# Graph convolution stage of a four-layer graph network: the product of gathered rows moved to the head of the iteration, the steps behind it one block later, reciprocal roots taken for two blocks at once

## The chip, the cores and the metric

The kernel runs on one core of one Trainium2 chip. The metric is the device time of one execution in microseconds (us), lower is better; the time before is the median of three runs.

## The reference, cut to what matters

A residual stream `x` of 4096 nodes by 256 features passes through four graph layers over one sparse 4096 x 4096 adjacency. The stage of this case computes layer 1 and prepares layer 2:

```python
h = jnp.maximum(_layernorm(x, axis=-1), 0.0)
# layer 1: graph convolution
adj_hat = adj + jnp.eye(N)
adj_norm = adj_hat / jnp.sum(adj_hat, axis=1, keepdims=True)
x = x + jnp.tanh(adj_norm @ (h @ W) + b)
# layer 2: attention over the neighbours, four heads
h = jnp.maximum(_layernorm(x, axis=-1), 0.0)
Wh = (h @ W2.T).reshape(n, HEADS, D_K)          # and the scores Wh . a_l, Wh . a_r
```

## The kernel before, in words

The nodes are cut into 32 blocks of 128 rows (`NB = 32`, `P = 128`, `D = 256`). A block's row of the adjacency has few nonzero columns, so for each block it is packed into five chunks of 128 columns (`CHUNKS + 1`): four chunks of neighbours anywhere in the graph and the block's own diagonal chunk. Two neighbouring blocks share one spare chunk (`acx`, 64 rows for each). The matching rows of `h @ W` lie in DRAM (`v_d`), and four indirect DMAs a block, one a chunk, fetch them, plus one for the spare of two blocks (`vgx`). So the 32 blocks need 144 indirect DMAs. They are issued by GpSimd (POOL), all on line 889.

The kernel runs stage by stage: attention (layer 0) up to 2180 us, the graph convolution from about 2195 to 2445 us, the second attention layer up to about 2720 us, and a last sparse product up to the end. The diff touches the graph convolution. Its loop runs over `b`, with one block entering each turn. A turn of before does this, with `o = b - LAG` and `LAG = 2`:

- loads of `xr` (the stream), `ac`, `acx` and the block's own rows of `v_d` from SyncE's queue (SP), and the gathers `vg`, `vgx` from POOL. The pool `gcnadj` holds six buffers of each.
- `second.normalise(o)` (L2238, L2243): ScalarE (ACT) makes `h` of block `o`, TensorE (PE) transposes it into `pt`.
- `second.product(o - 1)` (L2254): PE multiplies the transposed `ht` by `w_gat` into `pv`.
- `across_targets(o - 3)` (L2297 to L2300): PE transposes 4 columns of `steep`, ACT copies them to `steep_t`, SP stores them.
- `second.turned(o)` (L2248): VectorE (DVE) copies `pt` to `ht`.
- `sparse_product` (L920, L921): PE multiplies the packed adjacency of block `b` by the gathered rows into `acc`.
- `second.store(o - 1)` (L2282 to L2292): three exponentials on ACT, two instructions on DVE, the store to `table_d`.
- `y` (L2334 on DVE, tanh L2337 on ACT), `masks` (L2338, L2340), the sum into `xr` (L2342) and `second.stats(b)` (L2209 to L2232) with the reciprocal root of the variance by Newton steps: 13 small DVE instructions with the shift.

The order of DVE, ACT and PE is the program's own (`manual_schedule` over those three). A scheduler places SP's and POOL's instructions. Each engine works its list in order. The second attention layer gathers from `table_d`, so its first gather waits for the last stores of this stage.

Of the kernel before, what the change touches and what calls it, by code (L numbers as in the profile page):

```python
# [63 lines left out]
F32 = mybir.dt.float32  # L64
BF16 = mybir.dt.bfloat16
I32 = mybir.dt.int32
U32 = mybir.dt.uint32
# [9 lines left out]
P = 128  # L77
N = 4096
D = 256
NB = N // P  # L80
DC = D // P
DA = 64
HEADS = 4
# [582 lines left out]
def fast_layers(  # L666
# [80 lines left out]
    v_d = [dram.tile([N + 1, D], F32, name=f"v{k}_d") for k in range(2)]  # L747
# [152 lines left out]
    def gathered(pool, v_d, b, width=0):  # L900

        v = pool.tile([P, CHUNKS + 1, max(width, v_d.shape[1])], F32, name="vg")[:, :, : v_d.shape[1]]
        nc.sync.dma_start(v[:, CHUNKS, :], v_d[b * P : (b + 1) * P, :])
        for k in range(CHUNKS):
            gather(v[:, k, :], v_d, main_index(column, k, b))
        return v
# [10 lines left out]
    def sparse_product(acc, b, ac, v, acx, vx):  # L917

        for k in range(CHUNKS + 1):
            nc.tensor.matmul(acc, ac[:, k, :], v[:, k, :], start=(k == 0), stop=False)  # L920
        nc.tensor.matmul(acc, acx[side(b)], vx[side(b)], start=False, stop=True)  # L921
# [6 lines left out]
    sm = layer0.enter_context(tc.tile_pool(name="sm", bufs=4))  # L928
    wk = layer0.enter_context(tc.tile_pool(name="wk", bufs=2))
    ps = layer0.enter_context(tc.tile_pool(name="ps", bufs=2, space=PSUM))  # L930
# [1214 lines left out]
    with ExitStack() as st:  # L2145
# [3 lines left out]
        with tc.manual_schedule(engines=MANUAL):  # L2149
            enter1(va1, s1, vg_pool)  # L2150
            for b in range(-1, NB + 4):
                period1(b)
                if b == -1:
                    for q in range(8):
                        bs = slice(q * NB // 8, (q + 1) * NB // 8)
# [18 lines left out]
    w_last = weights(res, last_w, "w_last")  # L2174

    w_gat = res.tile([P, DC, D + 2 * HEADS], F32, name="w_gat")
# [15 lines left out]
    scale = res.tile([P, NB], F32, name="scale")  # L2192
# [4 lines left out]
    class Projection:  # L2197


        def __init__(self, sm, wk, ps, w, put, group, width=D):  # L2200
            self.group = group
            self.sm, self.wk, self.ps, self.w, self.put, self.width = sm, wk, ps, w, put, width
            self.tiles = {}

        def stats(self, b):


            six = self.sm.tile([P, 6], F32, name="six")
            nc.vector.bn_stats(six, xr[:, b, :])  # L2209
            nc.vector.bn_aggr(spread_[:, b, :], six)  # L2210
            if b % self.group < self.group - 1:
                return
            bs = slice(b + 1 - self.group, b + 1)
            var = self.sm.tile([P, self.group], F32, name="var")
            nc.vector.tensor_scalar_add(var, spread_[:, bs, 1], LN_EPS)
            if self.group > 1:
                nc.gpsimd.tensor_tensor(scale[:, bs], var, minus_half[:, : self.group], op=ALU.pow)
                return
            y, t = scale[:, bs], self.sm.tile([P, 1], F32, name="t")
            bits = self.sm.tile([P, 1], U32, name="bits")  # L2220
            nc.vector.tensor_scalar(bits, var.bitcast(U32), 1, None, op0=ALU.logical_shift_right)
            nc.vector.tensor_scalar(y.bitcast(U32), bits, -1.0, 1597463007.0, op0=ALU.mult, op1=ALU.add)
            for _ in range(3):
                nc.vector.tensor_mul(t, y, y)
                nc.vector.scalar_tensor_tensor(t, t, -0.5, var, op0=ALU.mult, op1=ALU.mult)
                nc.vector.scalar_tensor_tensor(y, t, 1.5, y, op0=ALU.add, op1=ALU.mult)
            self.shifts(b)

        def shifts(self, b):
            if b % self.group == 0:  # L2230
# [31 lines left out]
    def to_table(wk, v_d):  # L2262
        def put(b, pv):
            v = wk.tile([P, D], F32, name="v")
            nc.scalar.copy(v, pv)
            nc.sync.dma_start(v_d[b * P : (b + 1) * P, :], v)

        return put
# [3 lines left out]
    with ExitStack() as st:  # L2272
        adj_pool = st.enter_context(tc.tile_pool(name="gcnadj", bufs=6))
        sm = st.enter_context(tc.tile_pool(name="gcnsm", bufs=4))
        wk = st.enter_context(tc.tile_pool(name="gcnwk", bufs=3))
        ps = st.enter_context(tc.tile_pool(name="gcnps", bufs=2, space=PSUM))

        def put(b, pv):
            tab = wk.tile([P, TW], F32, name="tab")
            heads = tab[:, :HW].rearrange("p (h d) -> p h d", h=HEADS)  # L2280
            sr = pv[:, D + HEADS :]
            nc.scalar.activation(heads[:, :, DK], sr, AF.Exp, scale=SLOPE)  # L2282
            nc.scalar.activation(tab[:, HW:], sr, AF.Exp, scale=1.0 - SLOPE)
            nc.scalar.activation(steep[:, b, :], pv[:, D : D + HEADS], AF.Exp, scale=1.0 - SLOPE)
            nc.vector.tensor_copy(scores[:, b, :], pv[:, D:])
            nc.vector.tensor_tensor(
                heads[:, :, :DK],
                pv[:, :D].rearrange("p (h d) -> p h d", h=HEADS),
                heads[:, :, DK:].to_broadcast([P, HEADS, DK]),
                op=ALU.mult,  # L2290
            )
            nc.sync.dma_start(table_d[b * P : (b + 1) * P, :], tab)  # L2292

        def across_targets(b):

            pt = ps.tile([HEADS, P], F32, name="pst", tag="pv")
            nc.tensor.transpose(pt, steep[:, b, :], ident)  # L2297
            t = wk.tile([HEADS, P], F32, name="steep_t")
            nc.scalar.copy(t, pt)
            nc.sync.dma_start(steep_d[b], t)  # L2300

        second = Projection(sm, wk, ps, w_gat, put, 1, D + 2 * HEADS)
        LAG = 2
        with tc.manual_schedule(engines=MANUAL):
            for b in range(NB + LAG + 3):
                o = b - LAG
                if b % 4 == 0 and b < NB:
                    for c in (0, 4) if b == 0 else (b + 4,):
                        if c < NB:
                            nc.sync.dma_start(xr[:, c : c + 4, :], blocks(x1_d)[:, c : c + 4, :])  # L2310
                if b < NB:
                    ac = adj_pool.tile([P, CHUNKS + 1, P], F32, name="ac")
                    nc.sync.dma_start(ac, adjc_d[b])
                    if b % 2 == 0:
                        acx = adj_pool.tile([P, P], F32, name="acx")
                        nc.sync.dma_start(acx, adjx_d[b // 2])
                        vx = gathered_spare(adj_pool, v_d[0], b)
                    vg = gathered(adj_pool, v_d[0], b)
                if 0 <= o < NB:
                    second.normalise(o)  # L2320
                if 0 <= o - 1 < NB:
                    second.product(o - 1)
                if 0 <= o - 3:
                    across_targets(o - 3)
                if 0 <= o < NB:
                    second.turned(o)
                if b < NB:
                    acc = ps.tile([P, D], F32, name="acc")
                    sparse_product(acc, b, ac, vg, acx, vx)
                if 0 <= o - 1 < NB:  # L2330
                    second.store(o - 1)
                if b < NB:
                    y = wk.tile([P, D], F32, name="y")
                    nc.vector.scalar_tensor_tensor(  # L2334
                        y, acc, rdeg[:, b : b + 1], bias, op0=ALU.mult, op1=ALU.add
                    )
                    nc.scalar.activation(y, y, AF.Tanh)  # L2337
                    nc.vector.tensor_scalar(masks[:, b], ac, 0.0, None, op0=ALU.is_gt)  # L2338
                    if b % 2:
                        nc.vector.tensor_scalar(masks_x[:, b // 2], acx, 0.0, None, op0=ALU.is_gt)  # L2340

                    nc.vector.scalar_tensor_tensor(  # L2342
                        xr[:, b, :], y, -1.0, xr[:, b, :], op0=ALU.add, op1=ALU.add
                    )
                    second.stats(b)
        nc.vector.tensor_reduce(
            mild, scores.rearrange("p b k -> p (b k)"), AX.X, ALU.max, apply_absolute_value=True
        )
        nc.vector.tensor_scalar(mild, mild, SCORE_MAX, None, op0=ALU.is_le)
# [3 lines left out]
    with ExitStack() as st:  # L2353
        tab_pool = st.enter_context(tc.tile_pool(name="gattab", bufs=5))
        u_pool = st.enter_context(tc.tile_pool(name="gatu", bufs=2))
        sm = st.enter_context(tc.tile_pool(name="gatsm", bufs=4))
        wk = st.enter_context(tc.tile_pool(name="gatwk", bufs=3))
        ps = st.enter_context(tc.tile_pool(name="gatps", bufs=2, space=PSUM))
        third = Projection(sm, wk, ps, w_last, to_table(wk, v_d[1]), 2)
        state = [{} for _ in range(NB)]  # L2360
        LAG = 6

# [92 lines left out]
        with tc.manual_schedule(engines=MANUAL):  # L2455
            for b in range(NB + LAG + 2):
                o = b - LAG
# [54 lines left out]
    with ExitStack() as st:  # L2512
        adj_pool = st.enter_context(tc.tile_pool(name="lastadj", bufs=6))
        wk = st.enter_context(tc.tile_pool(name="lastwk", bufs=3))
# [79 lines left out]
```

## Time and profile before

| what | before |
|---|---|
| median of three runs | 2910.83 us (2905.03 to 2912.14) |
| profiled execution, its own time | 2910.45 us |
| its span in the profile | 2908.7 us |
| busy in the span | PE 87%, DVE 80%, ACT 68%, POOL 38% |
| first gather of the stage starts | 2198.52 us |
| `y` of the first, second, last block starts | 2218.50, 2225.90, 2430.02 us |
| last gather of the stage starts | 2391.86 us |
| first gather of the next stage starts | 2444.68 us |

The busy shares are those of the whole span; they say little of this stage, which takes a twelfth of it. The stage is read from its own window: the waits in it, the order of time of one turn, and the pace of the gathers. PE's clock is granted in stretches at full or half speed; "PEclk" is the mean granted share.

### The profile page before, as it was taken

The numbers are of one execution on the slowest core, as the hardware profiler recorded it, in microseconds if no ns is written. First come the engines' busy times: TensorE is split into PE (matmuls) and PEld (weight loads), VectorE is DVE, ScalarE is ACT, GpSimd is POOL, SyncE is SP. The second block draws the span as 40 slices with busy tenths as digits, with TensorE's granted clock in tenths as the row PEclk, the third lists the DMA queues.
The fourth block names the chain that finished last, engine by engine and source line by source line (L and its number), as shares of the span: only waits on it lengthen the run. The fifth ranks groups of instructions, "written<-read, shape, count | busy, mean of one in ns | idle before, by whom it ended". The sixth has DMA issues, their size and how long they took to land. (4 is left out here: it accounts for less than half of the span.)

```text
span 2908.7 us, 43850 instructions
## 1 busy us (share of the span) xinstructions
PE 2523.0 (87%) x12359; PEld 1850.5 (64%) x12359; DVE 2312.7 (80%) x9516; ACT 1976.6 (68%) x3289; POOL 1098.0 (38%) x1152
## 2 busy tenths in 40 slices
PE   5769999999999884699999999999895776999777
PEld 4537777777777762467676766677773554788444
DVE  4799999999999866898989879999964765888200
ACT  2689999999999634887888878788520123999100
POOL 3200000000000001488888554344425752764476
PEclk7779999999999996899999999999996887999887
DMA  7611222222222113244444433334337653654576
GB/s 254 222 55 59 92 69 87 89 69 91 80 75 89 40 40 103 64 126 126 122 136 118 134 111 102 99 117 123 101 98 227 209 165 104 173 164 121 160 210 183
DMA packets 227371, 349.57 MB, mean 120 GB/s; under 512 B 34727, under 2 KB 160172, under 8 KB 227116
## 3 DMA queue, kind: packets, MB, share of 16 engines
q1 hardware_dynamic: 185820, 237.70, 25.7%
q0 software_dynamic: 40320, 108.72, 13.6%
q8 instruction: 101, 1.65, 0.2%
q14 instruction: 154, 1.26, 0.1%
q10 hardware_dynamic: 976, 0.23, 0.0%
HBM read 280.22 MB, written 66.28 MB: 119 GB/s over the span
## 5 line engine op out<-in xcount | busy, mean ns | idle before, releaser
L1269 ACT ACTIVATE unread<-e,next_pair 128x4096 uint8<-128x4096 f32 (+1 forms) x320 | 859.5, 2686 | 160.9 <-DVE next_pair L1365 109.0
L1619 PE MATMUL pa<-va,at 128*128 128x256 f32 x2048 | 495.2, 387 | 0.0
L1619 PE MATMUL pa<-h,at 128*128 128x256 f32 x2048 | 469.0, 379 | 0.1
L1619 PEld LDWEIGHTS pa<-va,at 128*128 128x128 f32 x2048 | 376.4, 193 | 65.4 <-issue 21.6
L1619 PEld LDWEIGHTS pa<-h,at 128*128 128x128 f32 x2048 | 376.6, 190 | 45.3 <-issue 0.5
L1483 DVE MAX8 best<-near 128x8 f32<-128x256 f32 x1024 | 394.6, 415 | 0.1
L1610 ACT COPY at<-pat 128x512 f32<-128x512 f32 x512 | 284.0, 577 | 135.3 <-PE pat L1604 135.1
L1236 PE MATMUL pl<-kt,qb 64*128 64x512 f32 x1024 | 280.4, 657 | 91.3 <-ACT e L1250 88.4
L1604 PE MATMUL pat<-ident,e 128*128 128x128 f32 x2048 | 305.0, 279 | 51.2 <-DVEq L1543 25.1
L1604 PEld LDWEIGHTS pat<-ident,e 128*128 128x128 f32 x2048 | 240.0, 142 | 139.1 <-DVEq L1543 47.8
L1485 POOL COPY eighth<-best 128x16 f32<-128x16 f32 x64 | 47.1, 736 | 722.7 <-DVE best L1483 711.7
L1250 ACT ACTIVATE e<-pl,minus_guess 128x1024 f32<-128x1024 f32 x256 | 284.3, 1125 | 26.8 <-PE pl L1236 26.7
L1475 DVE SCALAR_TENSOR_TENSOR near<-e,end_hi 128x4096 f32<-128x4096 f32 x64 | 286.6, 4477 | 0.1
L1535 DVE SCALAR_TENSOR_TENSOR e<-e,end_t 128x4096 f32<-128x4096 f32 x64 | 286.2, 4472 | 0.2 <-issue 0.2
L889 POOL DMA_INDIRECT vg<-v_d,column x256 | 243.4, 951 | 91.0 <-issue 67.7
L920 PE MATMUL acc<-vg,ac 128*128 128x256 f32 x640 | 215.9, 489 | 66.3 <-DMA vg<-v_d,column 29.6
L920 PEld LDWEIGHTS acc<-vg,ac 128*128 128x128 f32 x640 | 146.9, 247 | 132.1 <-issue 59.8
L1236 PEld LDWEIGHTS pl<-kt,qb 64*128 64x128 f32 x1024 | 89.8, 194 | 195.7 <-ACT e L1250 156.4
L889 POOL DMA_INDIRECT vg<-mixed_d,column x128 | 180.5, 1410 | 57.6 <-issue 32.4
L2407 PE MATMUL acc<-u,tabg 128*65 128x128 f32 x1280 | 170.2, 280 | 13.5 <-DVE u L2397 13.5
L889 POOL DMA_INDIRECT vg<-far_d,column x128 | 166.6, 1301 | 39.0 <-issue 38.1
L2394 ACT ACTIVATE u<-targets,tabg 128x128 f32<-128x128 f32 x544 | 162.1, 389 | 10.0 <-DMA targets_x<-steep_d 10.0
(608 smaller groups left out, 4427.7 us busy)
## 6 DMA issues: line engine op xcount, KB each, us to landing
adj<-in_adjt SPq DMA_DIRECT2D x128, 512.0 KB
ac<-adjc_d SPq DMA_DIRECT2D x64, 320.0 KB
adjc_d<-ac SPq DMA_DIRECT2D x32, 320.0 KB
vg<-v_d SPq DMA_DIRECT2D x64, 128.0 KB
targets<-steep_d SPq DMA_DIRECT2D x32, 256.0 KB
ac<-adjc_d SPq DMA_DIRECT2D x32, 256.0 KB
table_d<-tab SPq DMA_DIRECT2D x32, 132.0 KB
tabg<-table_d SPq DMA_DIRECT2D x32, 132.0 KB
```

The source lines that it names most:

```text
L889: nc.gpsimd.indirect_dma_start(out, None, rows, bass.IndirectOffsetOnAxis(ap=index, axis=0))
L920: nc.tensor.matmul(acc, ac[:, k, :], v[:, k, :], start=(k == 0), stop=False)
L1236: nc.tensor.matmul(pl[:, r, :], s["qb"][rows], kt[rows, j * 512 : (j + 1) * 512], start=True, stop=True,)
L1250: nc.scalar.activation(s["e"][:, j * 1024 : (j + 1) * 1024], pl.rearrange("p r c -> p (r c)"), AF.Exp, bias=minus_guess[:, b : b + 1], acc ...
L1269: nc.scalar.activation(unread[:, :width], s["e"][:, :width], func, bias=s["at"], scale=-1.0, accum_out=s["signs"] if func == AF.Sign else ...
L1475: nc.vector.scalar_tensor_tensor(near, s["e"], end["hi"][:, b : b + 1], s["e"], op0=ALU.is_lt, op1=ALU.mult, accum_out=s["low"])
L1483: nc.vector.max(best[:, k, :], near[:, k * (N // SEG) : (k + 1) * (N // SEG)])
L1535: nc.vector.scalar_tensor_tensor(s["e"], s["e"], last, s["e"], op0=ALU.is_ge, op1=ALU.mult, accum_out=s["held"])
L1604: nc.tensor.transpose(pt[:, k, :], s["e"][:, c * P : (c + 1) * P], ident)
L1610: nc.scalar.copy(at, s["pt", g])
L1619: nc.tensor.matmul(s["pa"], s["at", g][:, k, :], va[:, c, :D], start=(c == 0), stop=(c == NB - 1))
L2407: nc.tensor.matmul(s["acc"][:, h, :], s["tab"][:, k, h * (DK + 1) : (h + 1) * (DK + 1)], s["u"][:, k, h, :], start=(k == 0), stop=False,)
```

## The change

In a turn, the sparse product of block `b` comes first on PE, ahead of the transposition, the product and the small transposition of earlier blocks. Those now lag three blocks behind instead of two. `y` and the masks come ahead of `turned` and `store` on DVE, and `tanh` ahead of the three exponentials on ACT. The Newton steps work on two columns, once every two blocks.

```diff
-        def __init__(self, sm, wk, ps, w, put, group, width=D):
-            self.group = group
+        def __init__(self, sm, wk, ps, w, put, newton, width=D):
+            self.group, self.newton = 2, newton
...
-            if self.group > 1:
+            if not self.newton:
                 nc.gpsimd.tensor_tensor(scale[:, bs], var, minus_half[:, : self.group], op=ALU.pow)
                 return
-            y, t = scale[:, bs], self.sm.tile([P, 1], F32, name="t")
-            bits = self.sm.tile([P, 1], U32, name="bits")
+            y, t = scale[:, bs], self.sm.tile([P, self.group], F32, name="t")
+            bits = self.sm.tile([P, self.group], U32, name="bits")
...
-            self.shifts(b)
+            self.shifts(bs.start)
...
-        second = Projection(sm, wk, ps, w_gat, put, 1, D + 2 * HEADS)
-        LAG = 2
+        second = Projection(sm, wk, ps, w_gat, put, True, D + 2 * HEADS)
+        LAG = 3
...
+                if b < NB:
+                    acc = ps.tile([P, D], F32, name="acc")
+                    sparse_product(acc, b, ac, vg, acx, vx)
                 if 0 <= o < NB:
                     second.normalise(o)
                 if 0 <= o - 1 < NB:
                     second.product(o - 1)
                 if 0 <= o - 3:
                     across_targets(o - 3)
-                if 0 <= o < NB:
-                    second.turned(o)
-                if b < NB:
-                    acc = ps.tile([P, D], F32, name="acc")
-                    sparse_product(acc, b, ac, vg, acx, vx)
-                if 0 <= o - 1 < NB:
-                    second.store(o - 1)
                 if b < NB:
                     y = wk.tile([P, D], F32, name="y")
...
                     if b % 2:
                         nc.vector.tensor_scalar(masks_x[:, b // 2], acx, 0.0, None, op0=ALU.is_gt)
+                if 0 <= o < NB:
+                    second.turned(o)
+                if 0 <= o - 1 < NB:
+                    second.store(o - 1)
+                if b < NB:
                     nc.vector.scalar_tensor_tensor(
                         xr[:, b, :], y, -1.0, xr[:, b, :], op0=ALU.add, op1=ALU.add
                     )
                     second.stats(b)
...
-        third = Projection(sm, wk, ps, w_last, to_table(wk, v_d[1]), 2)
+        third = Projection(sm, wk, ps, w_last, to_table(wk, v_d[1]), False)
```

The instance `third` of the next stage keeps its two-block groups and its power on POOL; only the way it is asked for differs.

## The prediction, made before the changed kernel ran

> **What bounds the stage now.** I read the page for the share of the stage, then the waits inside it, then one turn in order of time, then the gathers, and last the same gathers in the kernel's final stage. The waits from 2210 to 2440 us (engine and line, what it waited for, us in total, times, longest):
>
> ```profile
> ACT y L2337 <- DVE y L2334: 148.1, 32, 35.4
> PEld pt L2243 <- ACT h L2238: 64.5, 32, 2.8
> DVE y L2334 <- PE acc L921: 54.4, 32, 8.6
> PE pt L2243 <- ACT h L2238: 51.2, 32, 2.4
> POOL vg L889 <- PE acc L920: 16.3, 11, 2.8
> PEld acc L920 <- DMA vg<-v_d,column: 4.1, 4, 2.4
> ```
>
> PE stands 51.2 us for `h`, 1.6 us in each turn, and almost never for a gather (4.1 us). POOL stands 16.3 us for PE to free a buffer. So PE's own chain sets the pace and the gathers run ahead of it. One turn shows the chain: PE first, then ACT over the same time.
>
> ```profile
> 2397.49 0.44 PE L2243 MATMUL pt<-ident,h 128*128 128x128 f32 x2 [1.58 <-ACT h L2238]
> 2397.77 1.06 PE L2254 MATMUL pv<-w_gat,ht 128*128 128x264 f32 x4
> 2398.66 0.27 PE L2297 MATMUL pst<-ident,steep 128*4 128x128 f32 x1
> 2398.77 2.32 PE L920 MATMUL acc<-vg,ac 128*128 128x256 f32 x10
> 2401.03 0.70 PE L921 MATMUL acc<-vgx,acx 64*128 64x256 f32 x2
> 2403.30 0.44 PE L2243 MATMUL pt<-ident,h 128*128 128x128 f32 x2 [1.58 <-ACT h L2238]
> ...
> 2402.34 0.42 ACT L2337 ACTIVATE y<-y 128x256 f32<-128x256 f32 x1 [2.89 <-DVE y L2334]
> 2402.66 0.59 ACT L2238 ACTIVATE h<-xr,shift,scale 128x256 f32<-128x256 f32 x1
> ```
>
> `acc` ends at 2401.73, DVE makes `y`, ACT its tanh, and only then `h`: `h` is behind tanh in ACT's list, although its data was ready long before. Then PE goes on at 2403.30. PE's work in a full-clock turn is 2397.49 to 2401.73 = 4.24 us; the turn takes 5.81. With the half-clock stretches the mean turn is (2430.02 - 2225.90) / 30 = 6.80 us over blocks 1 to 31.
>
> What comes next is the gathers. The windows of the stage, its end, and the final stage (PE, PEld, DVE, ACT, POOL busy, then PEclk, DMA share, GB/s):
>
> ```profile
> 2210.00:2392.00 182.00, 137.53 (x477) 95.88 (x476) 121.86 (x546) 33.00 (x141) 128.13 (x135) 0.82 0.71 218
> 2392.00:2430.00 38.00, 30.09 (x109) 21.10 (x107) 25.48 (x116) 7.12 (x34) 0.81 (x1) 0.85 0.09 31
> 2740.00:2880.00 140.00, 107.94 (x293) 62.85 (x292) 10.62 (x25) 0.00 (x0) 105.85 (x113) 0.78 0.73 217
> ```
>
> POOL's last gather starts at 2391.86; for 38 us more PE works off blocks that have landed. In the final stage, with the same 144 gathers and little PE work, the start of the first is 2719.15 and of the last:
>
> ```profile
> 2898.26 0.95 POOL L889 DMA_INDIRECT vg<-v_d,column  x1 [0.30 <-issue]
> 2902.99 0.42 DVE L2527 SCALAR_TENSOR_TENSOR y<-acc,xr 128x256 f32<-128x256 f32 x1 [4.62 <-PE acc L921]
> ```
>
> That is (2898.26 - 2719.15) / 143 = 1.2525 us a gather (0.95 busy, 0.30 between), 5.64 us a block of 4.5 gathers, and 4.7 us from the start of the last gather to the use of its block. This is the floor under the changed stage.
>
> **The change, part by part.** *The product first.* After the change PE has, in the 1.6 us in which it waited for `h`, the next block's product, which needs only gathered rows and a PSUM buffer that `y` of two blocks ago has freed. `h` comes at the head of ACT's turn, behind the exponentials of the turn before; its shift was finished a whole turn earlier. After PE's last step of a turn (`pst`), ACT has steep_t 0.26, tanh 0.42, three exponentials of about 0.15 and `h` 0.59, about 1.7 us, while PE has 2.9 us (full clock) of sparse product ahead of the next `pt`. So no wait on `h` is left. The whole wait would be worth up to 51 us, but the gathers allow less. Without any wait for PE, the last of the 144 starts at 2198.52 + 143 x 1.2525 = 2377.6, and the last `y` at 2382.3 by the final stage's 4.7 us. PE must also do pt, pv and pst between blocks; I add 1.7 us and take 2384. It was 2430.0: 46 us earlier.
>
> Does PE keep that pace? 4.24 us at full clock; at half clock about 8.2 (the product 2227.86 to 2233.36 = 5.5, pt to pst 2435.41 to 2438.07 = 2.7). At half clock for every second stretch the mean is 2 / (1/4.24 + 1/8.2) = 5.6 us, just the gathers' pace; at the stage's own 0.82 it is about 5.2. Here a rule speaks against the change. The trace shows the clock at 0.82 although PE's longest steady wait is 2 us. The Trainium skill, TensorE: Matmul & The Clock Gate, "HAM oscillation", asks only that no idle gap exceed some 3.4 us, by which the clock would be 1.0 and a turn 4.24; its section "A second HAM failure mode" says that frequent short idling makes the clock swing, and the change turns one gap a turn into several short waits for gathers. The trace sides with the second: the final stage, with such waits, has 0.78. By either rule PE needs 4.2 to 5.6 us and the sum stays; only a clock that stays half breaks it.
>
> *DVE.* 13 small instructions at about 0.19 us from start to start now run 16 times, not 32: 208 fewer, 40 us of DVE time. That is off the path: DVE waits 54.4 us for `acc` already. What it does on the path: in an odd turn DVE has y 0.48, masks 0.70, ht 0.42, then stands for the exponentials (behind pst, steep_t and tanh, 2.5 to 3.8 us after `acc` ends), then 0.15 + 0.41 + 0.43 + 0.61 and 2.5 of Newton: 6.5 to 7.8 us. The even turn has no Newton: 4 to 5.3. The pair, 10.5 to 13.1, stands against 11.3 of gathers; the upper end is for half clock throughout. `y` of the even block comes a little late, but PE needs its buffer only two products later. I cost this at nothing, and 13.1 / 2 = 6.55 if the cover fails.
>
> *SP and POOL.* The stores of block j move from turn j+3 to j+4 in SP's list (`steep` from j+5 to j+6). Loads behind them are 6 blocks ahead of use, so a turn's delay leaves over 4 turns; landing takes about 3.7 us for a gather. Cost nothing; POOL's list is unchanged but for a few spare gathers that stand a place or two earlier, behind a product that is six blocks old by then. The Trainium skill, GPSIMD Engine Reference, "Key points", warns that DVE instructions with two SBUF inputs (the sum into `xr` is one) contend with GpSimd: the gather mean is 0.954 us here and 0.947 the median of the final stage without DVE work, so 1 us in 144; I use the measured one.
>
> *The end.* The stage before needs 14.66 us from the last `y` (2430.02) to the next stage's first gather (2444.68). Now `y` to shift takes 6.7 instead of 4.64 (ht, scores and tab come ahead of the sum into `xr`, and wait for the exponentials), and two blocks, not one, have `h` behind that shift: one more pass of pt, pv, pst, 1.5 to 2.7 us, I take 2.1. So 14.66 + 2.1 + 2.1 = 18.9.
>
> *Sum.* 2384 + 18.9 = 2402.9 for the next stage's first gather instead of 2444.68: 41.8 us less. Nothing behind it is changed, and it starts with that gather, so the rest shifts whole. Against the profiled execution's 2910.45: 2868.7. That execution is 0.4 us from the median, so the figure stands for the median too.
>
> **The rivals.** *PE or the landings at 6.2 us a block* instead of 5.64: for it, the clock's swings and the nearness of 5.6 to 5.64; against it, a PE that is behind is never idle and so regains its clock. From block 5 (about 2240) 26 blocks at 6.2 give 2402, the next gather at 2421, 24 us less: 2887. Chance 0.10.
>
> *The wait is hidden anyway*: DVE's odd and even turns bind at 6.55 us, 8 us less over 31 turns, and the longer end returns 4: 2907, no change to be seen (0.3% is 8.7 us, about what a measurement of this kernel can tell). Against it: 13.1 holds only at half clock. Chance 0.04.
>
> *Half clock throughout, slower*: place, PE's short waits for single gathers; price, 8.2 us a block from block 2 (2231) gives 2469 for the last `y`, 2488 for the next gather, +43: 2954. It decides once over 78% of the time is at half clock (mean above 6.8, clock under 0.61). For it: 2196 to 2231 ran mostly at half clock with such waits. Against it: the final stage's 0.78. Chance 0.06.
>
> **How the numbers follow.** The forecast (0.80) is 2869, its own range 2862 (last gather used at once, end as before: -48) to 2878. Faster: 0.80 + 0.10; same 0.04; slower 0.06. The range 2860 to 2886 takes in the forecast and most of the first rival.
>
> **What would show it.** Right: PE no longer waits for `h`, but for gathers of `v_d`; gathers at 1.25 us without a wait for PE to the last, near 2378; last `y` near 2384; next stage's first gather near 2403; clock 0.75 to 0.9. Wrong: POOL still waiting for `acc` (PE is the bound), `y` spaced by 6.5 in pairs of unequal turns (DVE), a clock near 0.5, or a gather gap above 1.25.

## The result, and the profile after

The changed kernel takes 2869.89 us (median of four runs, 2865.41 to 2874.15) against 2911.05 us of the kernel before (four runs, 2905.03 to 2912.14): a ratio of 0.9863, with a 95% interval of 0.9842 to 0.9883, or 41.2 us less. The forecast was 2869.

The profiled execution of the changed kernel took 2874.15 us, its span is 2872.4. It is the longest of the four, 4 us over their median, so it shows 36 us less than the profile of before. Read by stages, the change of this stage is 40.0 us:

| start, us | before | after | predicted |
|---|---|---|---|
| first gather of the stage | 2198.52 | 2199.75 | |
| last gather of the stage | 2391.86 | 2381.03 | 2377.6 |
| last `y` | 2430.02 | 2386.68 | 2384 |
| first gather of the next stage | 2444.68 | 2405.96 | 2402.9 |
| first to last gather | 193.3 | 181.3 | 179.1 |
| last `y` to the next stage's first gather | 14.66 | 19.3 | 18.9 |
| first gather of the stage to first of the next | 246.2 | 206.2 | 204.4 |

The first gather comes 1.2 us later than before, and what lies behind the stage takes 466.4 us instead of 464.0. The change touches neither; these 3.7 us are less than the 8.7 us by which the four runs of the changed kernel differ.

The waits of the stage come first, as they did for before (engine and line, what it waited for, us in total, times, longest; 2200 to 2400 us). Only the waits that bear on the chain are shown:

```profile
PEld acc L920 <- DMA vg<-v_d,column: 33.8, 40, 2.0
POOL vg L889 <- issue: 31.4, 103, 0.3
DVE y L2330 <- PE acc L921: 22.6, 16, 2.9
PE acc L920 <- DMA vg<-v_d,column: 17.7, 27, 1.6
PEld pt L2243 <- ACT h L2238: 7.5, 5, 3.3
PE pt L2243 <- ACT h L2238: 5.3, 3, 2.9
POOL vg L889 <- PE acc L920: 1.5, 5, 0.3
```

PE's wait for `h` has fallen from 51.2 us in 32 turns to 5.3 us in three. In its place PE now waits for gathers, 17.7 us, and its weight load 33.8. (PE's multiplications and its weight loads, PEld, wait at the same time; the two sums overlap.) POOL has no stall: each of its entries is 0.3 us, the plain gap between two gathers, and the 16.3 us for which it waited for `acc` are down to five such gaps. So PE now follows the gathers, and they run to the end without waiting for PE:

```profile
2199.75 1.02 POOL L889 DMA_INDIRECT vgx<-v_d,column  x1 [16.25 <-DVE found L1594]
...
2381.03 0.95 POOL L889 DMA_INDIRECT vg<-v_d,column  x1 [0.30 <-issue]
...
2386.68 0.45 DVE L2330 SCALAR_TENSOR_TENSOR y<-acc,rdeg,bias 128x256 f32<-128x256 f32 x1
...
2405.96 0.94 POOL L889 DMA_INDIRECT tabg_x<-table_d,column  x1 [23.98 <-DMA steep_d<-steep_t]
```

One turn in order of time shows the new chain. It begins at the end of a block's product:

```profile
2329.81 0.61 ACT L2238 ACTIVATE h<-xr,shift,scale 128x256 f32<-128x256 f32 x1
2331.03 0.70 PE L921 MATMUL acc<-vgx,acx 64*128 64x256 f32 x2
2331.65 0.44 PE L2243 MATMUL pt<-ident,h 128*128 128x128 f32 x2
2331.93 1.06 PE L2254 MATMUL pv<-w_gat,ht 128*128 128x264 f32 x4
2332.82 0.27 PE L2297 MATMUL pst<-ident,steep 128*4 128x128 f32 x1
2332.93 0.61 PE L920 MATMUL acc<-vg,ac 128*128 128x256 f32 x2
2333.34 0.41 ACT L2333 ACTIVATE y<-y 128x256 f32<-128x256 f32 x1
...
2334.37 1.39 PE L920 MATMUL acc<-vg,ac 128*128 128x256 f32 x4 [0.83 <-DMA vg<-v_d,column]
...
2336.57 1.64 PE L920 MATMUL acc<-vg,ac 128*128 128x256 f32 x4 [0.81 <-DMA vg<-v_d,column]
```

`h` ends at 2330.42, before the product of this turn does. `pt` follows the product at once, without a bracket of idle time; before, it stood there for 1.58 us. The stop is now inside the next product, twice 0.8 us, each for a chunk of gathered rows. The window of the stage, with PE, PEld, DVE, ACT, POOL busy, PEclk, DMA share and GB/s, shows 548 matmuls in 170 us, where before had 477 in 182, and a higher clock (0.88, not 0.82):

```profile
2210.00:2380.00 170.00, 147.96 (x548) 95.80 (x549) 109.19 (x426) 34.80 (x160) 129.16 (x135) 0.88 0.78 237
```

### The profile page after: what moved, and what is told of

It reads as the page before. It is cut to its first block, busy times and chain, and to the rows that moved or that the text cites. A ratio compares the mean times of both kernels' runs of the same rounds, so it can differ in the third digit from the quotient of the medians.

```text
span 2872.4 us, 43628 instructions
## 1 busy us (share of the span) xinstructions
PE 2512.8 (87%) x12359; PEld 1838.6 (64%) x12359; DVE 2281.8 (79%) x9308; ACT 1973.6 (69%) x3289; POOL 1099.9 (38%) x1152
## 3 DMA queue, kind: packets, MB, share of 16 engines
q14 instruction: 153, 1.25, 0.1%
## 5 line engine op out<-in xcount | busy, mean ns | idle before, releaser
L1604 PE MATMUL pat<-ident,e 128*128 128x128 f32 x2048 | 306.2, 280 | 51.2 <-DVEq L1543 25.4
L920 PEld LDWEIGHTS acc<-vg,ac 128*128 128x128 f32 x640 | 133.0, 228 | 156.3 <-DMA vg<-v_d,column 72.8
L2408 PE MATMUL acc<-u,tabg 128*65 128x128 f32 x1280 | 170.5, 280 | 13.8 <-DVE u L2398 13.8
```

The lines of the kernel that those rows point to most:

```text
L1604: nc.tensor.transpose(pt[:, k, :], s["e"][:, c * P : (c + 1) * P], ident)
L2408: nc.tensor.matmul(s["acc"][:, h, :], s["tab"][:, k, h * (DK + 1) : (h + 1) * (DK + 1)], s["u"][:, k, h, :], start=(k == 0), stop=False,)
```

## The experiments

The change has three parts: the order of the turn, the lag with it, and the reciprocal roots of two blocks at once. The first set of four runs asks which of them carries the 41 us, and whether the order is needed as a whole. A second and a third set test the new bound. The medians of the first set are of four runs (`e2`: 20), in ratio to 23 runs of before (2909.60 us, 2900.81 to 2917.14).

**The order alone.** The changed kernel with a lag of two blocks and one root a turn, as before:

```diff
-            self.group, self.newton = 2, newton
+            self.group, self.newton = 1 if newton else 2, newton
...
-        LAG = 3
+        LAG = 2
```

> Only the order of the turn is changed; the lag stays two blocks and the reciprocal roots stay one block at a time. Theory (the gain is the wait of PE for h, cut down to the pace of the gathers; lag and paired roots only make room): PE has no wait for h of note, last gather starts near 2378 to 2382 us, last y near 2386, and the end of the stage is 2 us shorter than with the lag of three, so 2865 to 2873 us. Rival (the longer DVE turn binds: 13 small instructions in every turn, and y queued behind them, 6.5 us or more a turn): POOL waits for acc, turns of 6.5 us or more, 2890 to 2910 us.

Measured: 2870.53 us (2867.62 to 2873.87), ratio 0.9871 (0.9840 to 0.9903). That is the time of the changed kernel. Its waits, 2210 to 2388 us:

```profile
PEld acc L920 <- DMA vg<-v_d,column: 38.3, 38, 2.5
PE acc L920 <- DMA vg<-v_d,column: 22.5, 28, 2.1
...
PEld pt L2243 <- ACT h L2238: 5.9, 8, 1.4
...
PE pt L2243 <- ACT h L2238: 2.7, 4, 1.0
```

They are the waits of the changed kernel: gathers, and hardly any `h`. So the order is enough, and the rival, a DVE turn of 6.5 us or more, did not show: the mean turn from `y` to `y` is 5.4 us. The end of the stage is shorter than with a lag of three: 14.85 us from the last `y` to the next stage's first gather, instead of 19.3. That does not show in the median; in the profile the slower gathers of this kernel (183.6 us from the first to the last) and a later last `y` take 3.7 of the 4.5 us back.

**The other two parts alone.** The kernel before with `LAG = 3` and the paired roots, its turn in the old order (the diff of the change without the moved lines in the loop).

> Lag of three blocks and roots for two blocks at once, but the order of the turn as before. Theory: h is still behind tanh of the newest block in ACT's list, PE still waits 1.6 us a turn for it, turns stay 6.8 us, and the end is 2 to 4 us longer: 2910 to 2916 us, although DVE loses 40 us of work. Rival (the freed DVE time or the lag brings part of the gain): 2870 to 2900 us.

Measured: 2910.10 us (2900.87 to 2917.64), ratio 1.0000 (0.9990 to 1.0011). The waits, 2210 to 2440 us:

```profile
PEld pt L2243 <- ACT h L2238: 65.6, 32, 3.6
DVE y L2334 <- PE acc L921: 59.0, 29, 4.0
PE pt L2243 <- ACT h L2238: 52.4, 32, 3.2
...
POOL vg L889 <- PE acc L920: 16.3, 9, 2.8
```

They are the waits of before, in all 32 turns, and the last gather starts 194.0 us after the first. With the old order the longer lag and the 40 us of DVE work saved buy nothing. The longer end is there as well (18.3 us), 3.6 over before; this profile took 2915.9 us, above its median, and an interval that reaches to +3.2 us can't confirm so small a term.

**The pairs taken back.** The changed kernel with a lag of three and one root a turn (the first line of the diff of `e1`).

> The changed kernel with roots taken one block at a time again (twice the small DVE instructions), new order and lag of three kept. Theory (DVE is covered, about 5.3 us of packed work against 5.64 us of gathers a turn): 2868 to 2876 us, DVE nearly without idle time. Rival (the DVE turn of 6.5 to 7.8 us that the prediction named for odd turns now comes in every turn): 2890 to 2910 us, y evenly late, POOL waiting for acc.

Measured: 2871.96 us (2870.57 to 2874.74), ratio 0.9874 (0.9843 to 0.9906). The 208 small DVE instructions are back, about 40 us of DVE's time, and the total is within 2.1 us of the changed kernel, less than either kernel's runs spread. They lie beside other work. DVE is nearly without idle time, as was expected: in the 150 us from 2230 to 2380 it waits for 10.1 us, against 39.1 in the changed kernel. That room is what the paired roots give; the stage does not need it.

**One instruction moved.** The kernel before, in its old order, a lag of two, single roots. The only change is that ACT makes `h` of the block that the next turn transposes just ahead of this turn's tanh.

```diff
-        def normalise(self, b):
-            h = self.wk.tile([P, D], F32, name="h")
+        def lifted(self, b):
+            h = self.tiles[b] = self.wk.tile([P, D], F32, name="h")
...
+        def normalise(self, b):
+            if b not in self.tiles:
+                self.lifted(b)
+            h = self.tiles[b]
...
+                    if 0 <= o + 1 < NB:
+                        second.lifted(o + 1)
```

> The kernel before with one thing moved: ACT makes h of the next turn just ahead of tanh of this one; order on PE and DVE, lag and roots as before. Theory (what cost 1.6 us a turn was h's place behind tanh in ACT's list, not the place of the product on PE): PE's wait for h goes, gathers bind at 5.64 us a block, 2866 to 2876 us. Rival (the product has to come first on PE to cover h, because h of the lag of two comes only just in time after the roots): h waits for its shift, PE still waits over 0.7 us a turn, 2885 to 2910 us.

Measured: 2863.41 us (2860.94 to 2867.44), ratio 0.9843 (0.9810 to 0.9876): the whole gain without moving the product. The time is the theory's, even a little under it; the wait is the rival's, for PE still stops for `h` in each turn, and `h` waits for its shift. A turn in order of time:

```profile
2324.77 0.60 ACT L2238 ACTIVATE h<-xr,shift,scale 128x256 f32<-128x256 f32 x1 [2.79 <-DVE shift L2232]
...
2325.33 0.47 DVE L2339 SCALAR_TENSOR_TENSOR y<-acc,rdeg,bias 128x256 f32<-128x256 f32 x1
...
2325.42 0.44 PE L2248 MATMUL pt<-ident,h 128*128 128x128 f32 x2 [1.17 <-ACT h L2238]
...
2325.90 0.42 ACT L2344 ACTIVATE y<-y 128x256 f32<-128x256 f32 x1 [0.53 <-DVE y L2339]
...
2330.68 0.47 DVE L2339 SCALAR_TENSOR_TENSOR y<-acc,rdeg,bias 128x256 f32<-128x256 f32 x1
...
2330.76 0.44 PE L2248 MATMUL pt<-ident,h 128*128 128x128 f32 x2 [1.12 <-ACT h L2238]
```

The stop is 1.1 us instead of 1.58, and the turn at full clock 2330.76 - 2325.42 = 5.34 us instead of 5.81. That is the smaller part of the gain. The larger part is PE's clock. In the kernel before it falls to half for 3.4 us at a time, in every turn or every second one; here it stays full from 2233 to 2386.5 (columns as above; first before as a whole, then some of its turns, cut where the granted clock changes, and last `e4`):

```profile
2233.10:2433.00 199.90, 152.63 (x557) 108.03 (x556) 141.67 (x634) 39.70 (x174) 111.41 (x117) 0.85 0.55 169
2318.40:2328.70 10.30, 7.15 (x33) 5.03 (x32) 7.09 (x30) 2.24 (x8) 7.67 (x8) 1.00 0.62 180
2328.70:2332.10 3.40, 3.40 (x10) 2.55 (x9) 2.47 (x14) 0.43 (x4) 2.77 (x3) 0.50 0.77 238
2332.10:2335.50 3.40, 1.82 (x9) 1.04 (x9) 1.83 (x5) 0.91 (x2) 2.01 (x3) 1.00 0.56 169
2335.50:2338.90 3.40, 3.40 (x11) 2.52 (x10) 2.91 (x18) 0.43 (x4) 2.50 (x3) 0.50 0.71 211
2233.00:2386.50 153.50, 121.31 (x545) 87.30 (x544) 135.76 (x615) 41.73 (x173) 109.31 (x115) 1.00 0.73 216
```

From block 1 to 31 the mean turn falls from 6.80 to 5.34 us. PE's own work in it falls from 152.63 / 199.9 x 6.80 = 5.19 us to 121.31 / 153.5 x 5.34 = 4.22, and the rest of the turn from 1.61 to 1.12. By this estimate 1.0 of the 1.5 us is the clock's and 0.5 the shorter stop's; at the clock of before the turn would be 5.19 + 1.12 = 6.3 us. In the changed kernel, with a mean turn of 5.36, the same sum gives PE 147.96 / 170 x 5.36 = 4.67 us of work: 0.5 us from the clock and 0.9 from the stop. Both come of the one move, since nothing else was changed in `e4`; what the move is worth at an unchanged clock, no run shows.

Nor do the gathers decide from there on, as was expected. PE hardly waits for a gather (2205 to 2395 us), and DVE hardly for PE (last line, DVE alone, 2230 to 2380):

```profile
PE pt L2248 <- ACT h L2238: 36.7, 30, 3.8
PEld acc L920 <- DMA vg<-v_d,column: 2.1, 3, 1.2
PE acc L920 <- DMA vg<-v_d,column: 0.5, 1, 0.5
DVE y L2339 <- PE acc L921: 1.0, 1, 1.0
```

That 1.0 us is the only wait of DVE that the view lists in these 150 us. From 2235 us on, `y` follows `y` every 5.28 to 5.41 us: in `e4` DVE's list is full and sets the turn, and PE's stop for `h` is the time in which DVE finishes the shift. Since 5.3 us is less than the 5.64 of a block's gathers, the work only uses up their lead: `y` starts 11.6 us behind the start of its block's last gather in the second block and 7.7 in the last, where the final stage needs 4.7. The two bounds end within 3 us of each other.

The kernels beside one another, from one profile each:

| kernel | first to last gather, us | last gather to last `y` | last `y` to next gather | stage | median |
|---|---|---|---|---|---|
| before | 193.3 | 38.2 | 14.7 | 246.2 | 2911.05 |
| after | 181.3 | 5.7 | 19.3 | 206.2 | 2869.89 |
| `e1` order alone | 183.6 | 7.1 | 14.9 | 205.5 | 2870.53 |
| `e2` lag and pairs alone | 194.0 | 38.1 | 18.3 | 250.4 | 2910.10 |
| `e3` without pairs | 182.5 | 8.3 | 18.6 | 209.3 | 2871.96 |
| `e4` `h` ahead of tanh | 180.6 | 7.7 | 13.8 | 202.1 | 2863.41 |

The four quick kernels come within 4.5 us of the 179.1 that 143 gathers need at 1.2525 us. That says only that nothing held POOL up; what the rest of the stage follows is said by the waits. In the changed kernel, `e1` and `e3` PE waits for gathers (17.7, 22.5 and 20.7 us), so they bind there. In `e4` DVE binds. It is close in `e1` and `e3` too: in stretches of both, `y` follows `y` every 5.19 us with hardly a wait of DVE.

**Fewer gathers.** To test that bound directly, the fourth gather of each block was replaced by a plain load, in the changed kernel and in the kernel before, with the changed kernel and `e4` run again beside them.

```diff
-                    vg = gathered(adj_pool, v_d[0], b)
+                    vg = adj_pool.tile([P, CHUNKS + 1, D], F32, name="vg")
+                    nc.sync.dma_start(vg[:, CHUNKS, :], v_d[0][b * P : (b + 1) * P, :])
+                    nc.sync.dma_start(vg[:, CHUNKS - 1, :], v_d[0][b * P : (b + 1) * P, :])
+                    for k in range(CHUNKS - 1):
+                        gather(vg[:, k, :], v_d[0], main_index(column, k, b))
```

> The changed kernel with the fourth of a block's gathers in this stage replaced by a plain load of the same size on SP (the block's own rows once more), so that chunk's product is of other rows; 112 gathers instead of 144. Theory (the pace of the changed stage is set by the issue of gathers at 1.25 us each): the gathers now need 4.4 us a block, the stage speeds up until PE (4.2 to 5 us) or the DVE pair (10.5 / 2 = 5.25 us) binds, 15 to 22 us over the stage: 2846 to 2858 us, POOL waiting for acc. Rival (PE or DVE already binds in the changed stage, or the transfers themselves): 2866 to 2874 us.

> The kernel before with the same replacement of one gather a block by a plain load on SP (again that chunk's product is of other rows). Theory (the chain through tanh and h binds before, the gathers run ahead): no change, 2904 to 2915 us, POOL only waits longer for acc. Rival (gathers also held back the stage before): 2885 to 2900 us.

> The changed kernel once more, beside the next run on one chip. Theory: 2866 to 2874 us.

> The kernel before with only h moved ahead of tanh on ACT, once more, beside the changed kernel. Theory (same pace of gathers, but the end keeps the lag of two, 4 us shorter): 2862 to 2868 us, 3 to 7 us below the changed kernel. Rival (the difference seen was scatter between calls): the two within 2 us.

In this set and in the one that repeats it every kernel, the one before too, took about 3.1 ms, 7 to 9% longer than above. They ran on two other chips than the first set (the record numbers the chips 8, 0 and 13); whether the chips are the cause is open. The four of the second set were then run once more:

> The changed kernel with the fourth of a block's gathers in this stage replaced by a plain load on SP of the block's own rows (that chunk's product is of other rows), again, because in the call before every kernel, the one before the change too, took about 3.1 ms[...]. Theory (issue of gathers sets the pace of the changed stage): 15 to 22 us below the changed kernel, 2846 to 2858 us, with POOL done early and the next bound PE or the DVE pair at 5 to 5.25 us a block. Rival (PE, DVE or the transfers bind already): within 4 us of the changed kernel.

> The kernel before with the same replacement (that chunk's product is of other rows), again for the same reason. Theory (before the change the chain through tanh and h binds): no change, 2904 to 2915 us, POOL waits for acc longer than the 16 us of before. Rival (gathers or landings held the stage back before, too): 10 to 25 us faster.

> The changed kernel once more, beside the next run on one chip, again for the same reason. Theory: 2866 to 2874 us, or the same ratio to before, 0.984 to 0.988.

> The kernel before with only h moved ahead of tanh on ACT, once more, beside the changed kernel. Theory (same pace of gathers, end with a lag of two, 4 us shorter): 2862 to 2868 us, 3 to 7 us below the changed kernel. Rival (the difference of the first call was scatter): the two within 2 us.

| kernel | second set, us | ratio | third set, us | ratio (95%) |
|---|---|---|---|---|
| before | 3137.57 | | 3125.78 | |
| `e7` after | 3108.65 | 0.9919 | 3100.03 | 0.9921 (0.9895 to 0.9947) |
| `e8` `h` ahead of tanh | 3112.75 | 0.9924 | 3102.34 | 0.9929 (0.9902 to 0.9956) |
| `e5` three gathers, after | 3064.61 | 0.9774 | 3056.80 | 0.9778 (0.9746 to 0.9811) |
| `e6` three gathers, before | 3113.05 | 0.9929 | 3104.83 | 0.9934 (0.9911 to 0.9956) |

Here the gain of the change is 0.8%, not 1.4%. The windows by stretches of time say where these runs lose (the changed kernel in the profile of the result, then the same kernel in the third set, `e7`; columns as above):

```profile
0.00:1000.00 1000.00, 896.41 (x4422) 661.40 (x4423) 923.33 (x3783) 868.33 (x1240) 54.59 (x165) 0.94 0.31 100
1000.00:2000.00 1000.00, 879.35 (x4251) 647.61 (x4249) 847.23 (x3839) 743.66 (x991) 538.91 (x471) 0.95 0.36 106
```

```profile
0.00:1000.00 1000.00, 896.85 (x4459) 661.85 (x4460) 926.95 (x3807) 870.73 (x1243) 54.59 (x165) 0.96 0.31 100
1000.00:2000.00 1000.00, 765.67 (x3568) 553.06 (x3567) 723.21 (x3253) 635.30 (x833) 426.40 (x415) 0.88 0.31 91
```

The first millisecond, in which POOL is busy for 55 us only, is the same in both (PE 896 us). In the second, with the gathers of the layer before, PE does 114 us less. A stretch of this stage from the second set shows what such a loss is made of:

```profile
2372.66 0.70 PE L922 MATMUL acc<-vgx,acx 64*128 64x256 f32 x2
...
2374.42 0.95 POOL L890 DMA_INDIRECT vg<-v_d,column  x1 [0.30 <-issue]
2379.47 0.48 DVE L2331 SCALAR_TENSOR_TENSOR y<-acc,rdeg,bias 128x256 f32<-128x256 f32 x1 [14.24 <-remote]
2379.70 0.94 POOL L890 DMA_INDIRECT vgx<-v_d,column  x1 [4.33 <-remote]
...
2379.98 0.42 ACT L2334 ACTIVATE y<-y 128x256 f32<-128x256 f32 x1 [15.90 <-DVE y L2331]
```

From 2375.4 to 2379.5 PE, POOL, DVE and ACT stand still together. DVE had its input earlier (two products had ended by 2373.4), and POOL waited for nothing that the program lists; "remote" is no engine of the kernel. That spoils the test. In the third set the three gathers take 43 us off the changed kernel (3100.03 to 3056.80), over the 15 to 22 that were expected. By the profiles 36 of them fall in this stage (245.7 to 209.3 us from its first gather to the next stage's) and 7 behind it, where the kernels are the same; POOL is relieved of 32 x 1.25 = 40 us. But in the rerun without the replacement the last `y` already comes 20.8 us behind the last gather, not 5.7 as in the first set: there the gathers were not the pace, and the test can't speak for the first set. And the kernel before, for which no change was expected, gains 21 us (25 in the second set). The direct test of the bound is inconclusive. Under the conditions of the first set it was not made.

The reruns of the changed kernel and of `e4` tie: `e4` is 4.1 and 2.3 us behind, within the spread. So the 6.5 us by which it leads in the first set are not confirmed.

## Why the prediction was right, step by step

*`h` stands behind tanh.* Right. The wait is nearly gone, the stage is 40 us shorter, and `e1` and `e2` put the gain in the order alone. The cause is narrower than the prediction had it: it credited the product at the head of the turn, which covers the wait. `e4` leaves the product where it was, moves one instruction on ACT, and has the whole gain. The cause was the place of `h` in ACT's list; putting the product ahead is one way around it. What the prediction left out is that PE's own work gets faster with the stop gone, 4.7 us a turn instead of 5.2 (estimated above). Its sum did not need that: 5.2 was under the gathers' 5.64.

*The gathers take over as the floor.* Supported, by PE's waits for `vg` in three kernels, by POOL without a stall, and by a last `y` 5.65 us behind the last gather. The direct test did not settle it. Taken to the letter, one sign of being wrong came true, a gather gap above 1.25. The term that was mis-sized is the gather itself: 1.2677 us from start to start, not 1.2525, or 2.2 us over 143. POOL's idle time between two is unchanged at 0.30; the difference is in the gathers' own duration. Most take 0.95 us as in the final stage, but 12 of the 144 take 1.05 to 1.27, together 2.2 us over 0.95. The longest, and one in the profile of `e1`:

```profile
2363.10 0.48 DVE L2334 TENSOR_SCALAR masks<-ac 128x640 bf16<-128x640 f32 x1
2363.13 1.27 POOL L889 DMA_INDIRECT vg<-v_d,column  x1 [0.31 <-issue]
2363.50 0.42 DVE L2248 COPY ht<-pt 128x256 f32<-128x256 f32 x1
```

```profile
2289.18 0.48 DVE L2334 TENSOR_SCALAR masks<-ac 128x640 bf16<-128x640 f32 x1
2289.35 1.13 POOL L889 DMA_INDIRECT vg<-v_d,column  x1 [0.30 <-issue]
```

In `e1` all 22 long gathers (3.9 us over) and in `e3` all 18 (3.1 us) lie beside `masks` and the copy `ht` that follows it; in the changed kernel 9 of the 12 lie beside `masks`, 8 of these beside `ht` too. Not every gather in that place is long: of those that touch both, 22 of 28 in `e1`, 18 of 27 in `e3` and 8 of 27 in the changed kernel are. In `e4`, where other work stands between the two, there are two long gathers (0.5 us). With these sums the floor of 179.1 becomes 181.3, 183.0, 182.2 and 179.6, against 181.3, 183.6, 182.5 and 180.6 measured. The prediction had weighed contention between DVE and POOL and allowed 1 us for it, from the sum into `xr`; the long gathers cost 2 to 4 us, and they go with `masks` and `ht`. That is read from overlap in the traces; no run took `masks` away, so contention stays an argument.

*PE keeps the pace.* Right: 0.88 is within the 0.75 to 0.9 named. The fear that many short waits would pull the clock down did not come true; the direction was the other way, 0.82 before, 0.88 after, 0.91, 0.94 and 0.95 in `e3`, `e1` and `e4`. The sum did not rest on it.

*DVE costs nothing.* Right. The instructions fell by 208 (9516 to 9308), and `e3` brings them back for 2.1 us, within the spread. In the changed kernel's odd turn at 2331.7 DVE needs 6.5 us from `acc` to the shift, in the even turn after it 4.9 to its last instruction; 6.5 to 7.8 and 4 to 5.3 were named. It costs nothing, but by little: with single roots DVE needs 5.19 us a turn in `e1` and `e3`, against 5.64 of gathers.

*SP and POOL cost nothing.* Right, by POOL's gaps of 0.30 to the last gather.

*The end.* 19.3 us from the last `y`, 18.9 named; `e1` and `e4` with a lag of two have 14.9 and 13.8, `e2` and `e3` with three have 18.3 and 18.6. So the longer lag costs 4 us there, as worked out. The last `y` comes 5.65 us behind the last gather, 6.4 named: the granted clock was full there (1.00 from 2375 to 2391.7 us).

*The rivals.* PE or the landings at 6.2 us a block: no, the mean turn from block 1 to 31 is 5.36. DVE at 6.55: no; the turns are unequal, as that rival had them, but DVE waits for PE's `acc` in them, and `e3` adds its work at no cost. Half clock throughout: no, 0.88.

*The number.* Part of its closeness is luck. The stage came out 1.8 us longer than worked out (206.2, not 204.4), and the median, within 1 us of the forecast, is one of runs that spread over 8.7 us.

## What to carry to other kernels

An engine works its list in order, so look at the instruction that another engine waits for and ask when its own data was ready; if that was long before, its place in the list is the fault, and moving one instruction can be worth as much as a new schedule. Then work out the next bound before counting the whole wait as gain: 51 us of waits, with a faster clock on top, were worth 41, because 4.5 gathers take 5.64 us whatever PE does. A wait need not vanish: in `e4` PE still stops for 1.1 us a turn, and it costs nothing once DVE's turn is the longer one. And look at where the next two bounds lie: here the gathers at 5.64 us and DVE at 5.2 to 5.3 are so close that kernels with different bounds end at the same time, and an equal time alone does not show a common bound.

## What the runs showed of the hardware that was not expected

The granted clock of PE rose when its stops became shorter or moved: from 0.82 in the stage to 0.88 after, 0.91 in `e3`, 0.94 in `e1` and 0.95 in `e4`. In `e4` the stop is of the same kind as before, one a turn, but 1.1 us instead of 1.58, and the clock stays full for 153 us where before it fell to half for 3.4 us at a time. Less idle time does not go with a higher clock among these four: PE of the changed kernel is idle least (0.7 us a turn, estimated above, against 1.1 in `e4`), and its clock is the lowest. What sets the clock is open.

A gather of 128 rows issued by POOL took 1.05 to 1.27 us instead of 0.95 in 48 of the 82 cases in which it touched DVE's `masks` and the `ht` behind it (`e1`, `e3` and the changed kernel).

Two sets of runs took 7 to 9% longer for every kernel, with standstills of several engines at once (4 us above). In the changed kernel's profile of the third set there are none beyond those of the first set up to 1000 us, where POOL is busy for 55 us only, and 18 of over 1 us in the next 1000. What causes them stays open. In these sets the gain of the change is 0.8%; how long the standstills are in the kernel before is not known, as there is no trace of it from those sets.
